# Attention in a fused attention and non-local block: scores and value products in quarter tiles, block by block

## The chip, the cores and the metric

The kernel runs on one core of a Trainium2 chip. A core has TensorE (matrix products, named PE in the profile; its weight loads are PEld), VectorE (DVE), ScalarE (ACT), GpSimd (POOL) and SyncE (SP), whose queue starts most transfers. The metric is the device time of one execution in microseconds.

## The reference

Eight images of 512 channels and 32 x 32 positions (N = 1024) go through two layers, all in 32-bit floats. Layer 0 is attention with 8 heads of 64 channels; layer 1 is a non-local block without softmax, followed by a normalization over the whole batch.

```python
q, k, v = (conv1x1(x, W, b).reshape(B, 8, 64, 1024) for W, b in ((Wq, bq), (Wk, bk), (Wv, bv)))
attn = softmax(einsum('bhdn,bhdm->bhnm', q, k) * 64 ** -0.5)
x = x + conv1x1(einsum('bhnm,bhdm->bhdn', attn, v), Wp, bp)
theta, phi, g = (conv1x1(x, w, b).reshape(B, 256, 1024) for w, b in ...)
y = einsum('bcd,bdn->bcn', einsum('bcn,bdn->bcd', theta, phi) / 1024, g)
z = conv1x1(y, W_w, W_b) + x
out = (z - mean(z)) * rsqrt(var(z) + 1e-5) * gamma + beta     # mean and variance per channel, over the batch
```

## The kernel before

**Products with weights.** Each 1x1 convolution (q, k, v, project, theta with phi, g, and the last product z of the first images) is done as seven block products instead of eight, on quarters of the weight matrix and of the data, with sums and differences of quarters made beforehand. `seven` (line 169) runs them in the order of the table `SEVEN` (line 165): each entry names the weight block, the data block, the PSUM slot 0 to 2 that it adds onto, the output quarter that is read from the slot after it, and whether that read is the first of its quarter (`first`, mostly on ScalarE) or is added to it (`add`, on VectorE). Two entries with one slot accumulate in it, so the second waits until the slot was read. `data_sums` (line 151) makes the data's four sums on VectorE in four blocks of the ring. `load_w` (line 114) loads the next weights, with two weight buffers.

**PSUM.** Three slots of two banks (`s0` to `s2`, pool `psS`) are given out in turn, to `seven` and to the scores. Two slots of one bank (pool `psO`) take the value products, the denominators and a few small products.

**Attention** (line 281). A pair of heads has its 2 x 64 channels on the 128 partitions. A unit is a pair of heads and one half of the 1024 query positions: 8 units. A step is a unit and one of 8 blocks of 128 keys: 64 steps per image. A step's scores (line 303) are two products of 64 channels by 128 keys with 512 queries, one per head, each in one half of the array's rows (tiles of 64 rows x 128 columns), each into its own PSUM bank; ScalarE takes exp of both banks at once into a ring block (line 306), and VectorE adds the block to the unit's running sum (lines 310, 312). A step's value products (lines 335 to 338) are two products of 128 keys by 64 channels with 512 queries, one per head, each in one half of the array's columns (tiles of 128 rows x 64 columns), accumulated over the 8 steps of the unit in one bank, which ScalarE copies out (line 378).

**Order.** The steps are cut into runs of six (`RUN`, the last has four). The order on TensorE is written out by hand (`pe` keeps it): scores of run i, then value products of run i - 1. The first value product of a run is split at column 128 (`LEAD`). The scores of the next image's q (`before_last`) come ahead of the last run's value products, its v (`after_last`) behind the denominators. VectorE, ScalarE and the queues are ordered by a planner that works with its own estimates of durations and when things are due.

**Softmax's denominators.** Of four units the running sums are spread by transfers (`spread`, four of 128 KB per unit) into one tile; VectorE folds it with three additions (`fold`), one product with a matrix of ones (`denominators`) sums it over the partitions, VectorE takes the reciprocal, a transfer to memory and broadcasts bring it back, and VectorE multiplies the four units' outputs with it (`normalize`). The first four units' denominators are done within attention, the other four's after it. In the last image the last four units take a short way each, without spreading (`normalize_alone`: a product with ones, a reciprocal, a multiplication).

**Per image**: attention, v and k of the next image, project with its residual, theta and phi, g, f, z. The first image's q, k and v come ahead of all; the last three images' z, the statistics and the outputs come at the end (`last_z`).

## Time and profile before

| | us |
|---|---|
| median of 3 runs (2222.07 to 2223.56) | 2223.41 |
| the profiled execution's own time | 2223.11 |
| its span, first to last instruction | 2221.3 |
| TensorE busy | 2187.9 |
| VectorE busy | 1285.3 |
| ScalarE busy | 703.3 |
| score products, L303, busy | 462.7 |
| value products, L338, busy | 458.6 |
| exp, L306: 512 of 1.040 | 485.8 |
| additions to the running sums, L312: 384 of 1.225 | 470.3 |

Busy time is the time in which an engine has at least one instruction under way; matmuls overlap, so the mean of one (0.599 for L303) times its count is more than the busy time. A row of the groups gives line, engine, operation, what is written and read, the tile of the array (rows * columns) and the count; a row of the timeline gives start, length and the same. Each product in the program leaves two matmul records and two weight-load records. The granted TensorE clock was 0.994 of full speed in the mean.

### The profile page before, as it was taken

Reading aid. Unit: us, or ns where it says so; the run is one execution under the profiler, and the core shown is the slowest. Engines: PE = TensorE matmul, PEld = TensorE weight load, DVE = VectorE, ACT = ScalarE, POOL = GpSimd, SP = SyncE. Lnnn points to the kernel's source line nnn. Section 1 sums busy time; section 2 is a strip of 40 time slices with the busy share of each in tenths; the row PEclk is TensorE's granted clock in tenths of the full one; section 3 lists DMA queues with packets and bytes.
Section 4 is the critical chain, followed back from the end, with each engine's and each line's share of the span. In section 5 each row is a group of like instructions: output and inputs, shape, how many; then the busy total and the mean of one; then the engine's idle time right before and its main releaser. Section 6 shows DMA issues by size and latency. Waiting matters only on the chain.

```text
span 2221.3 us, 21043 instructions
## 1 busy us (share of the span) xinstructions
PE 2187.9 (98%) x8314; PEld 1111.1 (50%) x8314; DVE 1285.3 (58%) x1231; ACT 703.3 (32%) x823; POOL 35.4 (2%) x36
## 2 busy tenths in 40 slices
PE   8999999999999999999999999999999999999996
PEld 3634664346643456335563355633656346643362
DVE  4576446764477644775447754477543674547736
ACT  1453103531045310452105521065102541045215
POOL 0000000000000000000000000000000000000000
PEclk9999999999999999999999999999999999999998
DMA  6212223122131221412223221232234122132347
GB/s 237 86 24 82 106 100 128 28 76 100 60 128 45 74 86 63 134 43 80 72 92 104 62 67 69 90 105 62 67 129 144 29 62 90 67 106 58 137 159 304
DMA packets 58235, 208.56 MB, mean 94 GB/s; under 512 B 10385, under 2 KB 16785, under 8 KB 52753
## 3 DMA queue, kind: packets, MB, share of 16 engines
q1 hardware_dynamic: 56752, 206.09, 28.0%
q8 instruction: 67, 1.10, 0.2%
q10 hardware_dynamic: 1376, 1.05, 0.1%
q14 instruction: 40, 0.32, 0.0%
HBM read 129.12 MB, written 46.53 MB: 79 GB/s over the span
## 4 chain that ended last, share of the span: by engine, by line
PE 97%; DVE 1%; DMA 0%; ACT 0%; issue 0%; DVEq 0%
PE ps L303 21%; PE po L338 18%; PE pv L189 9%; PE pq L189 9%; PE ptp L189 9%; PE pk L189 9%; PE pp L189 9%; PE pg L189 4%; PE pf L437 2%; PE pz L189 2%; PE pz L536 2%; PE po L336 1%; PE pwf L456 1%; PE po L335 1%; PE den L338 1%; DVE x L485 0%
## 5 line engine op out<-in xcount | busy, mean ns | idle before, releaser
L306 ACT ACTIVATE e<-ps 128x1024 f32<-128x1024 f32 x512 | 485.8, 1040 | 328.1 <-PE ps L303 286.4
L312 DVE TENSOR_TENSOR acc<-acc,e 128x1024 f32<-128x1024 f32 x384 | 470.3, 1225 | 156.5 <-ACT e L306 124.8
L303 PE MATMUL ps<-q,k 64*128 64x512 f32 x2048 | 462.7, 599 | 0.0
L338 PE MATMUL po<-e,v 128*64 128x512 f32 x1872 | 458.6, 595 | 0.0
L303 PEld LDWEIGHTS ps<-q,k 64*128 64x128 f32 x2048 | 187.8, 186 | 272.7 <-issue 164.2
L338 PEld LDWEIGHTS po<-e,v 128*64 128x64 f32 x1872 | 148.0, 137 | 214.9 <-issue 205.7
L446 ACT ACTIVATE g<-pg,gb 128x512 f32<-128x512 f32 x32 | 22.0, 687 | 427.2 <-PE pg L189 427.2
L189 PE MATMUL pp<-t_o,w_WpT 128*128 128x512 f32 x256 | 115.7, 600 | 1.9 <-DVE x L407 1.9
L310 DVE TENSOR_TENSOR acc<-e,e 128x1024 f32<-128x1024 f32 x64 | 77.7, 1214 | 65.4 <-ACT e L306 61.7
L189 PE MATMUL pq<-t_x,w_WqT 128*128 128x512 f32 x256 | 113.9, 593 | 1.5 <-DVE q L206 1.5
L189 PE MATMUL pv<-w_WvT,t_x 128*128 128x256 f32 x512 | 114.5, 379 | 0.0
L189 PE MATMUL ptp<-w_tp,t_x 128*128 128x256 f32 x512 | 114.4, 379 | 0.0
L189 PE MATMUL pk<-t_x,w_WkT 128*128 128x512 f32 x256 | 113.8, 592 | 0.0
L206 DVE TENSOR_TENSOR k<-k,pk 128x1024 f32<-128x1024 f32 x24 | 29.3, 1222 | 143.6 <-PE pk L189 143.6
L189 PEld LDWEIGHTS ptp<-w_tp,t_x 128*128 128x128 f32 x512 | 97.4, 190 | 13.1
L189 PEld LDWEIGHTS pv<-w_WvT,t_x 128*128 128x128 f32 x512 | 97.3, 190 | 13.0
L251 ACT ACTIVATE q<-pq,bq 128x512 f32<-128x512 f32 x64 | 40.5, 683 | 180.3 <-PE pq L189 180.3
L189 PE MATMUL pq<-x,w_WqT 128*128 128x512 f32 x192 | 89.9, 613 | 6.0 <-DMA w_WqT<-in_WqT_dram 6.0
L251 ACT ACTIVATE k<-pk,bk 128x512 f32<-128x512 f32 x64 | 40.5, 683 | 153.6 <-PE pk L189 153.6
L189 PE MATMUL pp<-o,w_WpT 128*128 128x512 f32 x192 | 88.7, 605 | 0.0
L189 PE MATMUL pv<-w_WvT,x 128*128 128x256 f32 x384 | 87.5, 381 | 0.0
L189 PE MATMUL ptp<-w_tp,x 128*128 128x256 f32 x384 | 86.8, 379 | 0.0
(131 smaller groups left out, 2007.0 us busy)
## 6 DMA issues: line engine op xcount, KB each, us to landing
fold<-acc SPq DMA_DIRECT2D x240, 128.0 KB, 2.4
x<-in_x_dram SPq DMA_DIRECT2D x32, 512.0 KB, 5.7
r<-den_d SPq DMA_DIRECT2D x120, 128.0 KB, 3.0
w_WqT<-kept_WqT SPq DMA_DIRECT2D x7, 1792.0 KB, 7.3
w_WvT<-kept_WvT SPq DMA_DIRECT2D x7, 1792.0 KB, 7.3
w_WkT<-kept_WkT SPq DMA_DIRECT2D x7, 1792.0 KB, 6.9
w_WpT<-kept_WpT SPq DMA_DIRECT2D x7, 1792.0 KB, 7.0
w_tp<-kept_tp SPq DMA_DIRECT2D x7, 1792.0 KB, 7.3
```

The source lines that it names most:

```text
L189: pe(nc.tensor.matmul(to_ps, lhsT(k), rhs(k), start=(s, at) not in begun, stop=(k == nk - 1), skip_group_check=True))
L206: nc.vector.tensor_tensor(at, at, ps, ALU.add)
L251: nc.scalar.activation(t[:, c, cols(q)], ps[:, m, :], AF.Identity, bias=bias[:, c:c + 1])
L303: pe(nc.tensor.matmul(ps[:, j, :], k[r, p, m * P:(m + 1) * P], q[r, p, h * 512:(h + 1) * 512], start=True, stop=True))
L306: nc.scalar.activation(e, ps, AF.Exp, scale=SCALE)
L310: nc.vector.tensor_tensor(accs[u], es[u, 0], e, ALU.add)
L312: nc.vector.tensor_tensor(accs[u], accs[u], e, ALU.add)
L335: pe(nc.tensor.matmul(to[:, :LEAD], l, r[:, :LEAD], start=start, stop=False, skip_group_check=True))
L336: pe(nc.tensor.matmul(to[:, LEAD:], l, r[:, LEAD:], start=False, stop=stop, skip_group_check=True))
L338: pe(nc.tensor.matmul(to, l, r, start=start, stop=stop, skip_group_check=True))
L437: pe(nc.tensor.matmul(ps[:, c, :], tp[:, i, c * P:(c + 1) * P], tp[:, i, CI:], start=(i == 0), stop=(i == NB - 1)))
L536: pe(nc.tensor.matmul(ps[:, h, :], wf[:, d, oc * P:(oc + 1) * P], g[d][:, h * 512:(h + 1) * 512], start=(d == 0), stop=(d == IC - 1)))
```

## The change

Scores and value products are both cut into tiles of 64 rows x 64 columns, four products each per step. For the scores the block of 128 keys is cut into two halves (`c`), which go to the two halves of the array's columns; each head keeps its half of the rows and its bank. For the value products the 128 keys are cut into two halves (`r`), which go to the two halves of the rows, each with its own bank; the heads keep their halves of the columns. The two banks of a unit are added at its end: ScalarE copies the first out, VectorE adds the second to it.

There are no runs. For each step TensorE does the scores of step i, then the value products of step i - 2 (`LAG`). All eight PSUM banks form four slots of two banks, given out in turn; in attention, scores use two of them in turn and the units' value products the other two. The small products take the next slot.

The next image's data sums are made near the end of attention, its q after the end, then both denominators, then v, then both normalizations (in order among themselves on VectorE). The fold follows right after the spread of its fourth unit, and the first one ends in a tile of its own (`fold1`); the ring has 10 blocks instead of 11. In the last image, the first four units' denominators and the short ways of the other units stand at steps 46, 54 and 62 and behind the end. `seven` gets a second order (`EARLY`, for the first q and the last project): block product "12" second, the read of "21" started from the slot of "s3t3", and "t4" in a slot of its own.

The diff, without the lines that only rename a pool or a slot:

```diff
-    RUN = 6
-    LEAD = 128
+    LAG = 2
...
-    ring = ctx.enter_context(tc.tile_pool(name="ring", bufs=11))
-    psS = ctx.enter_context(tc.tile_pool(name="psS", bufs=1, space=PSUM))
-    psO = ctx.enter_context(tc.tile_pool(name="psO", bufs=2, space=PSUM))
+    fold1 = ctx.enter_context(tc.tile_pool(name="fold1", bufs=1))
+    ring = ctx.enter_context(tc.tile_pool(name="ring", bufs=10))
+    psum = ctx.enter_context(tc.tile_pool(name="psum", bufs=1, space=PSUM))
...
-    SEVEN = (("11", 0, "11", 0, "11", True), ("s1t1", 3, "t1", 1, "22", True), ("s2t2", 4, "t2", 0, "12", True),
-             ("s4", 6, "22", 1, "12", False), ("s3t3", 5, "t3", 0, "22", False), ("12", 1, "21", 2, "11", False),
-             ("t4", 2, "t4", 0, "21", True))
-
-    def seven(name, w, data, positions_out, first, add, between=None, order=(0, 1, 2, 3, 4, 5, 6)):
+    SEVEN = (("11", 0, "11", 0, (("11", True),)), ("s1t1", 3, "t1", 1, (("22", True),)),
+             ("s2t2", 4, "t2", 0, (("12", True),)), ("s4", 6, "22", 1, (("12", False),)),
+             ("s3t3", 5, "t3", 0, (("22", False),)), ("12", 1, "21", 2, (("11", False),)),
+             ("t4", 2, "t4", 0, (("21", True),)))
+
+    EARLY = (SEVEN[0], SEVEN[5], *SEVEN[1:4], ("s3t3", 5, "t3", 0, (("22", False), ("21", True))),
+             ("t4", 2, "t4", 2, (("21", False),)))
+
+    def seven(name, w, data, positions_out, first, add, between=None, early=False):
 
 
 
         nk, half = w.shape[2], w.shape[3]
         tags = list(free)
+        free[:] = [tags[3], tags[1], tags[0], tags[2]] if early else [tags[3], tags[1], tags[2], tags[0]]
         slots, begun = {}, set()
-        for n, (what, wi, di, s, to, is_first) in enumerate(SEVEN[i] for i in order):
-            if s not in slots:
-                slots[s] = bank(tags[s], f"{name}_{s}")
+        for n, (what, wi, di, s, reads) in enumerate(EARLY if early else SEVEN):
+            if s not in slots or early and what == "t4":
+                slots[s] = bank(tags[s], f"{name}_{s}_{n}")
+                begun -= {one for one in begun if one[0] == s}
             ps, d = slots[s], data[di]
             if positions_out:
                 parts = [(ps.rearrange("p h (i f) -> p (h i) f", f=half)[:, i, :], i * half // 512,
@@ -189,10 +197,10 @@
                     pe(nc.tensor.matmul(to_ps, lhsT(k), rhs(k), start=(s, at) not in begun, stop=(k == nk - 1),
                                         skip_group_check=True))
                     begun.add((s, at))
-            (first if is_first else add)(to, ps)
+            for to, is_first in reads:
+                (first if is_first else add)(to, ps)
...
-        free[:] = [tags[1], tags[2], tags[0]]
...
-                nc.scalar.activation(t[:, c, cols(q)], ps[:, m, :], AF.Identity, bias=bias[:, c:c + 1])
+                if how.get("early") and q == "21":
+                    nc.vector.tensor_scalar(t[:, c, cols(q)], ps[:, m, :], bias[:, c:c + 1], 1.0, ALU.add, ALU.mult)
+                else:
+                    nc.scalar.activation(t[:, c, cols(q)], ps[:, m, :], AF.Identity, bias=bias[:, c:c + 1])
...
+    def columns(ps, lhsT, rhs):
+
+        for j in range(2):
+            pe(nc.tensor.matmul(ps[j * D:(j + 1) * D, :], lhsT, rhs(j), start=True, stop=True, skip_group_check=True))
...
-        def scores(run):
-            for u, m in run:
-                p, h = units[u]
-                ps = next_bank(f"ps_{b}_{u}_{m}")
+        def scores(i):
+            u, m = steps[i]
+            p, h = units[u]
+            ps = bank(tags[i % 2], f"ps_{b}_{u}_{m}")
+            for j in range(2):
+                r = slice(j * D, (j + 1) * D)
+                for c in range(2):
+                    keys = slice(m * P + c * P // 2, m * P + (c + 1) * P // 2)
+                    pe(nc.tensor.matmul(ps[c * P // 2:(c + 1) * P // 2, j, :], k[r, p, keys],
+                                        q[r, p, h * 512:(h + 1) * 512], start=True, stop=True, skip_group_check=True))
+            e = block(f"e_{b}_{u}_{m}")
+            nc.scalar.activation(e, ps, AF.Exp, scale=SCALE)
+            es[u, m] = e
+            if m == 1:
+                accs[u] = w3.tile([P, 2, 512], F32, tag="acc", name=f"acc_{b}_{u}")
+                nc.vector.tensor_tensor(accs[u], es[u, 0], e, ALU.add)
+            elif m > 1:
+                nc.vector.tensor_tensor(accs[u], accs[u], e, ALU.add)
+            if m == NB - 1 and u not in alone:
+                spread(u)
+
+        def weighted(i):
+            u, m = steps[i]
+            p, _ = units[u]
+            if m == 0:
+                sums[u] = bank(tags[2 + u % 2], f"po_{b}_{u}")
+            ps, e = sums[u], es.pop((u, m))
+            for r in range(2):
+                keys = slice(r * P // 2, (r + 1) * P // 2)
                 for j in range(2):
-                    r = slice(j * D, (j + 1) * D)
-                    pe(nc.tensor.matmul(ps[:, j, :], k[r, p, m * P:(m + 1) * P], q[r, p, h * 512:(h + 1) * 512],
-                                        start=True, stop=True))
-                e = block(f"e_{b}_{u}_{m}")
-                nc.scalar.activation(e, ps, AF.Exp, scale=SCALE)
-                es[u, m] = e
-                if m == 1:
-                    accs[u] = w3.tile([P, 2, 512], F32, tag="acc", name=f"acc_{b}_{u}")
-                    nc.vector.tensor_tensor(accs[u], es[u, 0], e, ALU.add)
-                elif m > 1:
-                    nc.vector.tensor_tensor(accs[u], accs[u], e, ALU.add)
-                if m == NB - 1 and u not in alone:
-                    spread(u)
+                    pe(nc.tensor.matmul(ps[j * D:(j + 1) * D, r, :], v[keys, m, (2 * p + j) * D:(2 * p + j + 1) * D],
+                                        e[keys, j, :], start=(m == 0), stop=(m == NB - 1), skip_group_check=True))
+            if m == NB - 1:
+                nc.scalar.copy(part(u), ps[:, 0, :])
+                nc.vector.tensor_tensor(part(u), part(u), ps[:, 1, :], ALU.add)
...
-        def fold(g):
-            t = folded[g]
-            for to, l in ((0, 1), (2, 3), (0, 2)):
-                nc.vector.tensor_tensor(t[:, to, :], t[:, to, :], t[:, l, :], ALU.add)
-
-        def columns(ps, lhsT, rhs, start, stop, lead):
-
-            for j in range(2):
-                to, l, r = ps[j * D:(j + 1) * D, :], lhsT(j), rhs(j)
-                if lead and j == 0:
-                    pe(nc.tensor.matmul(to[:, :LEAD], l, r[:, :LEAD], start=start, stop=False, skip_group_check=True))
-                    pe(nc.tensor.matmul(to[:, LEAD:], l, r[:, LEAD:], start=False, stop=stop, skip_group_check=True))
-                else:
-                    pe(nc.tensor.matmul(to, l, r, start=start, stop=stop, skip_group_check=True))
-
-        def denominators(g):
-
-            ps = psO.tile([P, 512], F32, tag="o", name=f"den_{b}_{g}")
+            if i == 3:
+                t = folded[g]
+                if g == 0:
+                    folded[g] = fold1.tile([P, 1, 1024], F32, tag="fold1", name=f"fold1_{b}")
+                for to, l, r in ((t[:, 0], t[:, 0], t[:, 1]), (t[:, 2], t[:, 2], t[:, 3]),
+                                 (folded[g][:, 0], t[:, 0], t[:, 2])):
+                    nc.vector.tensor_tensor(to, l, r, ALU.add)
...
-                nc.vector.tensor_tensor(part(4 * g + i), part(4 * g + i), r, ALU.mult)
-
-        def normalize_alone(u):
-            ps = psO.tile([P, 512], F32, tag="o", name=f"psum_{b}_{u}")
+                dve(nc.vector.tensor_tensor(part(4 * g + i), part(4 * g + i), r, ALU.mult))
...
-        def weighted(run):
-            lead = True
-            for u, m in run:
-                p, _ = units[u]
-                if m == 0:
-                    sums[u] = psO.tile([P, 512], F32, tag="o", name=f"po_{b}_{u}")
-                ps, e = sums[u], es.pop((u, m))
-                columns(ps, lambda j: v[:, m, (2 * p + j) * D:(2 * p + j + 1) * D], lambda j: e[:, j, :],
-                        m == 0, m == NB - 1, lead)
-                lead = False
-                if m == NB - 1:
-                    nc.scalar.copy(part(u), sums.pop(u))
-                    if u in alone:
-                        normalize_alone(u)
-
-        first = 4 * NB // RUN
-        d = None
-        for i, run in enumerate(runs):
-            scores(run)
-            if i == first + 1:
-                fold(0)
-            if i == first + 4:
+        for i in range(len(steps) + LAG):
+            if i < len(steps):
+                scores(i)
+            if i == len(steps) - 2:
+                near_end()
+            if i >= LAG:
+                weighted(i - LAG)
+            if alone and i in (46, 54, 62):
+                ps = bank(tags[3 - i // 8 % 2], f"psum_{i}")
+                if i == 46:
+                    d = denominators(0, ps[:, 1, :])
+                normalize_alone(i // 8 - 1, ps[:, 0, :])
+            if alone and i == 58:
                 normalize(0, d)
-            if i:
-                weighted(runs[i - 1])
-            if i == first + 2:
-                d = denominators(0)
-        before_last(lambda: None if alone else fold(1))
-        weighted(runs[-1])
-        d = None if alone else denominators(1)
-        after_last()
+        free[:] = tags
         if not alone:
-            normalize(1, d)
-        return o
+            return o, denominators, normalize
+        normalize_alone(7, next_bank("psum_7")[:, 0, :])
+        return o, None, None
...
-        seven(f"pp_{b}", w, data_sums(quarters_of(o), f"o_{b}"), False, first, add_to(xt), between)
+        seven(f"pp_{b}", w, data_sums(quarters_of(o), f"o_{b}"), False, first, add_to(xt), between,
+              early=b == B - 1)
...
-        def before_last(fold):
+        def near_end():
             if not last:
                 nxt["data"] = data_sums(quarters_of(nxt["x"]), f"x_{b + 1}")
-                fold()
-                nxt["q"], nxt["peak_q"] = heads_of(b + 1, "q", weights("WqT"), bq, nxt["data"])
-                load_w(nc.sync)
-
-        def after_last():
-            if not last:
-                nxt["v"] = values(b + 1, weights("WvT"), nxt["data"])
-                load_w(nc.sync)
-
-        o = attention(b, q, k, v, before_last, after_last)
+
+        o, denominators, normalize = attention(b, q, k, v, near_end)
         between = None
         if not last:
-            v = nxt["v"]
+            q, peak_q = heads_of(b + 1, "q", weights("WqT"), bq, nxt["data"])
+            load_w(nc.sync)
+            d = [denominators(g, next_bank(f"den_{b}_{g}")[:, 0, :]) for g in range(2)]
+            v = values(b + 1, weights("WvT"), nxt["data"])
+            load_w(nc.sync)
+            for g in range(2):
+                normalize(g, d[g])
```

## The prediction

> **What bounds the kernel now.** I read the page's busy shares and its chain first, then the TensorE timeline inside attention, then the same image cut into stages, then what TensorE waits for.
>
> ```profile
> PE 2187.9 (98%) x8314; PEld 1111.1 (50%) x8314; DVE 1285.3 (58%) x1231; ACT 703.3 (32%) x823; POOL 35.4 (2%) x36
> PE 97%; DVE 1%; DMA 0%; ACT 0%; issue 0%; DVEq 0%
> PE ps L303 21%; PE po L338 18%; PE pv L189 9%; PE pq L189 9%; PE ptp L189 9%; PE pk L189 9%; PE pp L189 9%; PE pg L189 4%; PE pf L437 2%; PE pz L189 2%; PE pz L536 2%; PE po L336 1%; PE pwf L456 1%; PE po L335 1%; PE den L338 1%; DVE x L485 0%
> ```
>
> TensorE carries 97% of the chain that ended last; the others work beside it. Only TensorE time can move the result. Its timeline around one pair of runs (start, length, operation, count):
>
> ```profile
> 698.80 1.89 PE L338 MATMUL po<-e,v 128*64 128x512 f32 x8
> 700.62 5.42 PE L303 MATMUL ps<-q,k 64*128 64x512 f32 x24
> 705.97 0.32 PE L335 MATMUL po<-e,v 128*64 128x128 f32 x1
> 705.98 0.64 PE L338 MATMUL po<-e,v 128*64 128x512 f32 x1
> 706.13 0.27 PE L335 MATMUL po<-e,v 128*64 128x128 f32 x1
> 706.24 0.49 PE L336 MATMUL po<-e,v 128*64 128x384 f32 x1
> 706.46 0.59 PE L338 MATMUL po<-e,v 128*64 128x512 f32 x1
> 706.56 0.49 PE L336 MATMUL po<-e,v 128*64 128x384 f32 x1
> 706.88 4.46 PE L338 MATMUL po<-e,v 128*64 128x512 f32 x20
> ```
>
> Each matmul leaves two records[...]. In single records inside a run the two tiles' first passes start 7 ns apart (701.151, 701.158), their second passes 0.429 us later, the next block another 0.429 later: one **half** is 0.4292 us, a block of scores or of value products two halves, 0.858. At the borders more goes by: from the last value half (700.087) to the second scores half (701.151) 1.064 instead of 0.858, so 0.206 lost; from the last scores half (705.443) to 706.883 1.440 instead of 1.287, so 0.153 lost. A pair of runs loses 0.36.
>
> Now the image by stages (attention up to its last run; next q; the last run and the denominators; next v):
>
> ```profile
> core 0: us, PE busy (x) PEld busy (x) DVE busy (x) ACT busy (x) POOL busy (x), PEclk, DMA share, GB/s
> 631.30:742.40 111.10, 111.10 (x522) 43.28 (x521) 83.61 (x74) 64.57 (x71) 0.00 (x0) 1.00 0.29 83
> 742.40:766.60 24.20, 24.20 (x58) 10.56 (x56) 13.25 (x12) 3.79 (x6) 0.00 (x0) 1.00 0.10 22
> 766.60:771.10 4.50, 4.50 (x24) 1.69 (x23) 2.65 (x3) 1.85 (x3) 0.00 (x0) 1.00 0.74 264
> 771.10:795.30 24.20, 24.20 (x114) 21.36 (x113) 13.11 (x11) 3.04 (x3) 0.00 (x0) 1.00 0.25 82
> ```
>
> Busy hides the borders (a matmul's record runs 0.16 us past its stream), so I take starts: 631.316 to 795.350 is 164.03 us. At full rate: 256 halves of attention 109.88, four of denominators 1.72, 56 of pq 24.03, 112 pv records at 0.2158 (the rate of ptp, 24.173/112) 24.17; 159.80 in all. **4.24 us per image are lost**, nearly all at borders. Other waits of TensorE:
>
> ```profile
> PE pq L189 <- DMA w_WqT<-in_WqT_dram: 6.0, 1, 6.0
> PE pp L189 <- DVE x L407: 1.9, 1, 1.9
> PE den L338 <- DVE ri L364: 1.8, 1, 1.8
> PE pq L189 <- DVE q L206: 1.5, 1, 1.5
> ```
>
> The last three are the last image's project, its denominators, and image 0's q.
>
> [...] the 512-wide L338 record of tile two starts at 705.98, before L335's second pass at 706.13, which stands ahead of it in the program. Four tiles at once no run here shows.
>
> **The change part by part.**
>
> *Quarter tiles, same halves.* A scores block becomes 4 matmuls of 64x64 tiles, as does a value block: 16 matmul and 16 load records per step instead of 8 and 8. If four tiles run together, a block still takes two halves. Resources, each against something shown. Moving data: 4 x 64 rows at once, as the value run's 2 x 128. PSUM writes: 4 x 64 partitions in two banks; scores now write 2 x 128. Weight loads: 64 columns keep a tile's loader about 55 ns (705.967 to 706.022), so four one after the other are 0.22 of a 0.429 half. Issue: at 650.589 TensorE's queue was empty after a wait, and the first loads of two successive matmuls came at 650.614 and 650.650: 36 ns per matmul, four per block 0.144 of 0.858. Order: a tile's second pass blocks that tile alone; passing one blocked record, as shown, already fills the array in a steady stream (two tiles one half behind the others). Cost taken: 0; bounds 0 to +0.429 per half (only two in flight), nothing below 0 since each tile streams 512 columns as before.
>
> *Borders.* All mode changes inside attention go (9 or 10 pairs, L335 split included). Left per image: into attention (0.1 of it in my window), into pq, into the two denominators between q and v, out of them: 0.1 + 3 x 0.2 = 0.7.
>
> *Start of attention.* Two score slots instead of three: scores(2) needs exp(0). Before, exp(0) began 1.236 after its scores' first matmul (902.724 to 903.960) and took 1.03; loads and matmul follow 0.1 later: ready at 2.37, wanted at 0.1 + 1.72 = 1.82; **+0.5**. Later scores(i) comes two steps (3.43) after scores(i-2), so 1.1 us spare, or 0.5 with the 0.585 output copy in between. Value products run two steps after their exp: not late.
>
> *VectorE, ScalarE, DMA.* ScalarE: 64.6 of 111 us busy. VectorE gains per unit an add of 128x512 from PSUM, at the 0.69 of L357: 8 x 0.7 = 5.5; second fold 3.7 moves in: 83.6 + 9.2 = 92.8 of 110. Cost 0, hidden by TensorE's 110; if that cover fails, see rival B. Normalize(0) (2 reciprocal of 3.36, 8 products) goes behind v: before, denominators at 770.1 gave normalized parts by 787.1; with 8 products about 9 us more, 796 to 800, wanted by project at 819. Its r loads on SP grow from 8 to 16 there, 3.0 us each, two buffers. Ring 11 to 10: value products and accumulation free blocks two to a few steps after exp. 0.
>
> So images 0 to 6: 159.8 + 0.7 + 0.5 = 161.0 instead of 164.03: **-3.0 each, -21.2**.
>
> *Last image*: first scores to ptp 148.11 (1963.43 to 2111.54). After: 109.88 + 5 column pairs x 0.858 = 4.29 + pp 24.03 = 138.2; entry and start 0.6; three mode excursions at steps 46, 54, 62 at 0.36 to 0.4, and the end 0.4: 1.6; at step 46 two reciprocals (6.7 us) read a slot that the value products of step 50 want about 6.2 us later, behind accumulation too: 1 to 3, take 2; leftovers 0.5. 142.9: **-5.2**. In it the early order of project: pp takes 28.01 now, 1.9 of it waiting and 1.7 more at half clock (0.5 for 3.41 us from 2093.995).
>
> *First q*: t4 gets its own slot and need not wait for the read of s3t3: **-1.5**, the row above.
>
> Sum -27.9. The profiled execution took 2223.11 (span 2221.3 and 1.8 around it), the median is 2223.41; from the median **2195.5 us**.
>
> **Rivals.**
>
> A, the sum above: 0.74, range 2186 to 2204 (lower if the start wait and the step-50 stall don't come, -6; half clock after that stall, +1.7, and borders of 0.3, +5 over the kernel).
>
> B, VectorE takes part of it back: a fold waiting for its spreads (2.4 us each) right behind the last one, queued accumulations, or r loads during v hold the slot of s3t3's read. For it: 84% filled in attention[...]. Against: ring of 10 covers some 8 steps, 13.7 us. 1 to 2.5 us per image: 2204 to 2215. 0.11.
>
> C, other side: quarter tiles do not all run at once. Place: every half of attention, 8 x 256 = 2048. If the two tiles that share rows must load in turn with the stream standing, 55 ns: +113, **2308**; two in flight, +879, 3075. It decides from 27.9/2048 = 14 ns per half. For it: no four-tile stretch in the trace. Against: the five resources above. 0.11.
>
> D, no change: the gain stands but scores wait for exp all along, as only two slots remain. A wait of 0.05 us per step (512) would eat 27.9. Against: 0.5 to 1.1 us spare. 2219 to 2228. 0.04.
>
> **Numbers.** About 0.2% (4.4 us) is what a measurement tells from no change. Faster A + B 0.85, same 0.04, slower 0.11. Range 2186 to 2215: A and B but for their ends, 0.8; the slower case lies outside.
>
> **What would show it.** Right: scores and value records of 64x64, four starts within about 30 ns, 0.429 between halves, about 110.5 from first scores to pq, no L335 rows; den between pq and pv. Wrong: halves over 0.443 us (C), gaps before scores with ScalarE as releaser (D) or before s3t3, t4 or first value products with VectorE (B); pp of the last image still near 28; step 50 of the last image stalling over 3 us.

## The result and the profile after

The changed kernel takes 2211.06 us (median of 6 runs, 2207.80 to 2211.89) against 2222.74 for the kernel before (6 runs, 2219.64 to 2226.62): ratio 0.9944, 95% interval 0.9931 to 0.9957. It is faster by 0.56%, or 11.7 us, where 27.9 us were forecast. The direction and the range were right, the size was not.

The page's busy shares and the chain of the changed kernel:

```profile
PE 2166.6 (98%) x12234; PEld 1066.1 (48%) x12234; DVE 1321.1 (60%) x1299; ACT 735.8 (33%) x821; POOL 35.4 (2%) x36
PE 93%; DMA 3%; DVE 2%; issue 1%; ACT 1%; SPq 0%; DVEq 0%; ACTq 0%
```

TensorE still carries the chain, but 7% of it now belongs to others, where it was 3%. Its timeline in the middle of attention (start, length, operation, count):

```profile
630.74 1.04 PE L346 MATMUL po<-e,v 64*64 64x512 f32 x8
631.60 1.04 PE L324 MATMUL ps<-q,k 64*64 64x512 f32 x8
632.46 1.04 PE L346 MATMUL po<-e,v 64*64 64x512 f32 x8
633.32 1.04 PE L324 MATMUL ps<-q,k 64*64 64x512 f32 x8
```

A block of eight records starts every 0.858 us, whether scores or value products. In single records (each product leaves two, called its first and second pass) the first passes of the four tiles start at 631.599, .606, .613 and .619, the second passes 0.429 later: four tiles run together in the 0.429 us that two tiles took before, and nothing is lost between the two kinds of product. The image's stages, attention, next q, the two denominators, next v:

```profile
core 0: us, PE busy (x) PEld busy (x) DVE busy (x) ACT busy (x) POOL busy (x), PEclk, DMA share, GB/s
627.50:738.10 110.60, 110.27 (x1025) 38.97 (x1024) 81.21 (x76) 68.81 (x71) 0.00 (x0) 1.00 0.26 72
738.10:762.30 24.20, 24.20 (x60) 10.56 (x56) 13.17 (x12) 4.38 (x7) 0.00 (x0) 1.00 0.10 22
762.30:764.20 1.90, 1.90 (x9) 0.48 (x8) 1.35 (x2) 1.27 (x2) 0.00 (x0) 1.00 0.62 106
764.20:788.50 24.30, 24.30 (x114) 21.39 (x113) 12.69 (x9) 3.04 (x3) 0.00 (x0) 1.00 0.30 112
```

By starts this is 160.97 us where it was 164.03, in each of the first seven images to within 0.06. So the core of the forecast holds, and the missing 16 us lie elsewhere. From the starts of matmuls in the two profiled executions (spans 2221.3 and 2209.6):

| stage | forecast | measured |
|---|---|---|
| first q | -1.5 | -1.6 |
| images 0 to 6, first scores to next k | -21.2 | -21.5 |
| image 0: bias products and project | 0 | +3.5 |
| k and project in images 1 and 6 | 0 | +1.3 |
| last image, first scores to end of project | -5.2 | +6.3 |
| the rest | 0 | +0.2 |
| sum | -27.9 | -11.8 |

The last image carries 11.5 of the missing us. TensorE there, at steps 46 to 48 and at the end of attention:

```profile
2023.88 1.04 PE L346 MATMUL po<-e,v 64*64 64x512 f32 x8
2024.85 1.08 PE L295 MATMUL psum<-fold,folds 128*64 128x512 f32 x4
2029.73 1.97 PE L295 MATMUL psum<-acc,ones 128*64 128x512 f32 x4 [3.81 <-DVE ri L373]
2031.63 1.99 PE L324 MATMUL ps<-q,k 64*64 64x512 f32 x8
2033.40 1.93 PE L346 MATMUL po<-e,v 64*64 64x512 f32 x8
...
2064.49 2.75 PE L346 MATMUL po<-e,v 64*64 64x512 f32 x24
2072.12 1.98 PE L295 MATMUL psum<-acc,ones 128*64 128x512 f32 x4 [4.88 <-DVE acc L333]
2074.03 5.14 PE L197 MATMUL pp<-o,w_WpT 128*128 128x512 f32 x8
```

Two things are to be seen. TensorE waits twice for VectorE, 3.8 and 4.9 us. And after each wait its products take twice as long: a scores block of 0.86 us takes 1.77 from start to next start (2031.63 to 2033.40). The record of the granted clock has two stretches of half speed here, 6.83 us each, from 2029.2 and from 2070.1. TensorE stood still for the first 0.6 and 2.0 us of them, and the rest cost it half its length: 3.1 and 2.4 us. Before, this image had one stretch, of 3.41 us. What VectorE did at the end:

```profile
2063.14 0.69 DVE L384 TENSOR_TENSOR o<-o,r 128x512 f32<-128x512 f32 x1 [0.85 <-DMA r<-den_d]
2063.75 3.88 DVE L333 TENSOR_TENSOR acc<-acc,e 128x1024 f32<-128x1024 f32 x3
2067.55 3.35 DVE L390 RECIPROCAL ri<-psum 128x512 f32<-128x512 f32 x1
2070.82 1.16 DVE L333 TENSOR_TENSOR acc<-acc,e 128x1024 f32<-128x1024 f32 x1
```

The last column product (a unit's running sum times the matrix of ones) needs the addition at 2070.82, which stands behind the additions that piled up behind a multiplication, and behind unit 6's reciprocal.

### The profile page after: what moved, and what is told of

Its sections match the earlier page's. It is cut to its first block, busy times and chain, and to the rows that moved or that the text cites. A ratio compares the mean times of both kernels' runs of the same rounds, so it can differ in the third digit from the quotient of the medians.

```text
span 2209.6 us, 28905 instructions
## 1 busy us (share of the span) xinstructions
PE 2166.6 (98%) x12234; PEld 1066.1 (48%) x12234; DVE 1321.1 (60%) x1299; ACT 735.8 (33%) x821; POOL 35.4 (2%) x36
## 4 chain that ended last, share of the span: by engine, by line
PE 93%; DMA 3%; DVE 2%; issue 1%; ACT 1%; SPq 0%; DVEq 0%; ACTq 0%
PE ps L324 19%; PE po L346 19%; PE pp L197 9%; PE pq L197 9%; PE ptp L197 9%; PE pv L197 8%; PE pk L197 6%; PE pg L197 4%; PE pf L449 3%; PE pz L197 2%; DMA r<-den_d 2%; PE pz L545 2%; PE pwf L468 1%; PE den L295 1%; ACT e L327 0%
## 5 line engine op out<-in xcount | busy, mean ns | idle before, releaser
L327 ACT ACTIVATE e<-ps 128x1024 f32<-128x1024 f32 x512 | 523.7, 1024 | 390.7 <-PE ps L324 383.1
L324 PE MATMUL ps<-q,k 64*64 64x512 f32 x4096 | 532.4, 591 | 2.6 <-ACT e L327 2.6
L346 PE MATMUL po<-e,v 64*64 64x512 f32 x4096 | 529.5, 590 | 0.0
L324 PEld LDWEIGHTS ps<-q,k 64*64 64x64 f32 x4096 | 155.0, 133 | 291.6 <-issue 278.9
L346 PEld LDWEIGHTS po<-e,v 64*64 64x64 f32 x4096 | 156.7, 133 | 283.9 <-issue 281.2
L384 DVE TENSOR_TENSOR o<-o,r 128x512 f32<-128x512 f32 x60 | 40.8, 689 | 91.0 <-DMA r<-den_d 91.0
L278 ACT COPY v<-pv 128x1024 f32<-128x1024 f32 x32 | 32.4, 1012 | 173.6 <-PE pv L197 173.6
```

What stands on the lines that cost most here:

```text
L278: seven(f"pv_{b}", w, data, True, lambda q, ps: nc.scalar.copy(at(q), as_v(ps)), lambda q, ps: nc.vector.tensor_tensor(at(q), at(q), as_v( ...
L324: pe(nc.tensor.matmul(ps[c * P // 2:(c + 1) * P // 2, j, :], k[r, p, keys], q[r, p, h * 512:(h + 1) * 512], start=True, stop=True, skip_gr ...
L327: nc.scalar.activation(e, ps, AF.Exp, scale=SCALE)
L346: pe(nc.tensor.matmul(ps[j * D:(j + 1) * D, r, :], v[keys, m, (2 * p + j) * D:(2 * p + j + 1) * D], e[keys, j, :], start=(m == 0), stop=(m ...
L384: dve(nc.vector.tensor_tensor(part(4 * g + i), part(4 * g + i), r, ALU.mult))
```

## The experiments

**The theory** after the result: quarter tiles give what was forecast; the loss is the order of the small steps around them, in the last image and in image 0, where TensorE waits for VectorE and then runs at half clock. **Rivals**: VectorE simply has too much to do there; the half clock belongs to the quarter tiles; and the gain comes from the new order rather than from the tiles. All runs were timed beside the kernel before. What is told of stages is read from each run's own profile.

**The tiles of before in the new order.** Scores in 64 x 128, value products in 128 x 64, all else as changed:

```diff
-                for c in range(2):
-                    keys = slice(m * P + c * P // 2, m * P + (c + 1) * P // 2)
-                    pe(nc.tensor.matmul(ps[c * P // 2:(c + 1) * P // 2, j, :], k[r, p, keys], ...
+                pe(nc.tensor.matmul(ps[:, j, :], k[r, p, m * P:(m + 1) * P], ...
...
-            for r in range(2):
-                keys = slice(r * P // 2, (r + 1) * P // 2)
-                for j in range(2):
-                    pe(nc.tensor.matmul(ps[j * D:(j + 1) * D, r, :], v[keys, m, ...], e[keys, j, :], ...
+            for j in range(2):
+                pe(nc.tensor.matmul(ps[j * D:(j + 1) * D, 0, :], v[:, m, ...], e[:, j, :], ...
...
-                nc.vector.tensor_tensor(part(u), part(u), ps[:, 1, :], ALU.add)
```

> Order, slots, lag and all else of the changed kernel, but the tiles of before: scores in 64 x 128, value products in 128 x 64, in one bank, without the addition of a second bank. Theory (the gain of 3.08 us per image comes from mode changes that the quarter tiles spare): each of 512 steps pays two mode changes, 0.36 us together, so 2211 + 184 = about 2395 us. Rival (the gain comes from the order block by block and the slots, and the tiles are beside the point): 2205 to 2225.

Measured: 2375.7 us, 1.0687 of before (1.0669 to 1.0705). Its timeline inside attention:

```profile
700.08 1.08 PE L342 MATMUL po<-e,v 128*64 128x512 f32 x4
701.09 1.13 PE L322 MATMUL ps<-q,k 64*128 64x512 f32 x4
702.15 1.08 PE L342 MATMUL po<-e,v 128*64 128x512 f32 x4
703.16 1.13 PE L322 MATMUL ps<-q,k 64*128 64x512 f32 x4
```

A step takes 2.07 us instead of 1.717: 0.35 for two mode changes (a mode change: TensorE goes from one tile shape to another). Attention is 132.25 us instead of 110.59, 0.338 per step over all 64, a little less than the 0.36 taken. The gain is the tile shape's; the new order with the old tiles costs 7%.

**Quarter tiles two steps at a time.** The same products in another order:

```diff
-            if i < len(steps):
+            if i % 2 == 0 and i < len(steps):
                 scores(i)
-            if i == len(steps) - 2:
-                near_end()
+                if i == len(steps) - 2:
+                    near_end()
+                scores(i + 1)
```

> Quarter tiles as changed, but TensorE does the scores of two steps and then the value products of two steps. Theory (with one tile shape the order makes no difference to TensorE): 2211 plus or minus 3, halves of 0.429 us as before. Rival (block by block is needed, since otherwise scores wait for exp with two slots): a wait of 0.2 us or more per pair of steps, 2260 or more.

Measured: 2207.17 us (0.9932; 0.9915 to 0.9948). Attention takes 110.65 us per image, against 110.59. With one tile shape the order made no difference to TensorE here, and two score slots suffice in both. The 4 us below the changed kernel's median is one more than expected: in this run's profile image 0's project had a half clock of 3.41 instead of 6.83 us, images 1 and 6 had no wait, and the last image took 152.0 us instead of 154.5.

**A slot of its own for the denominators in the last image.**

```diff
+            if alone and i == 38:
+                d = denominators(0, bank(tags[3], f"den_{b}_0")[:, 0, :])
             if alone and i in (46, 54, 62):
                 ps = bank(tags[3 - i // 8 % 2], f"psum_{i}")
-                if i == 46:
-                    d = denominators(0, ps[:, 1, :])
```

> The first four units' denominators of the last image move from step 46, where they share a slot with unit 4's column product, to step 38 and a slot of their own, which no value product wants before step 42. Theory (the shared slot makes TensorE wait 3.8 us for the reciprocal, and the wait halves the clock for 6.8 us): no wait at steps 38 and 46, no half clock after them; the last image's time from first scores to project falls from 128.9 to about 122.3 us, the kernel from 2211.1 to about 2204.5. Rival (VectorE is behind in this image, and TensorE waits for its reciprocals whatever slot they read): the wait goes along to steps 38 to 42, and the time falls by 0 to 2 us.

Measured: 2203.20 us, 0.9913 (0.9899 to 0.9927). TensorE at steps 38 and 46:

```profile
2009.08 1.08 PE L295 MATMUL den<-fold,folds 128*64 128x512 f32 x4
2010.09 1.09 PE L324 MATMUL ps<-q,k 64*64 64x512 f32 x8
...
2016.72 1.09 PE L346 MATMUL po<-e,v 64*64 64x512 f32 x8 [0.39 <-DVE ri L373]
...
2024.61 1.08 PE L295 MATMUL psum<-acc,ones 128*64 128x512 f32 x4
2025.62 1.09 PE L324 MATMUL ps<-q,k 64*64 64x512 f32 x8
```

The wait and the half clock behind it are gone, 0.4 us are left at step 42, and the last image takes 148.3 us instead of 154.5; the wait at the end, 4.6 us, stays. The rival falls: with the same reciprocals, at another step and on different slots, TensorE hardly waits. In the changed kernel the two column products wrote different banks of one slot, and the second waited for the reciprocal that read the first. Two separate tiles at step 46 itself weren't tried, so slot and step are not told apart.

**Less for VectorE near the end.**

```diff
-            if alone and i in (46, 54, 62):
+            if alone and i in (46, 54, 59):
...
-            if alone and i == 58:
+            if alone and i == 50:
                 normalize(0, d)
```

> In the last image unit 6's column product goes from step 62 to step 59, and the first four units' multiplications from step 58 to step 50; the shared slot at step 46 stays. Theory (at the end TensorE waits 4.9 us since VectorE does the reciprocal of unit 6 and four multiplications ahead of the last addition to unit 7's sum, and the wait halves the clock again): the wait before the last column product goes, project runs at full clock in 24.0 to 24.2 instead of 25.6 us, and the kernel falls from 2211.1 to about 2204. Rival (VectorE has too much to do in the last image, whatever the order): the wait stays above 3 us, and the kernel stays above 2208.

Measured: 2206.50 us, 0.9929 (0.9916 to 0.9943). The wait before the last column product shrinks from 4.9 to 2.4 us, and waits of 1.0 at step 58 (unit 7's value products, for unit 5's reciprocal) and 0.6 at step 59 appear; project takes 25.3 us, still partly at half clock. Both expectations missed: the order matters, but half of the wait stayed, so that VectorE's load in this image counts as well.

**All short ways as early as their slots allow.**

```diff
-            if alone and i in (46, 54, 62):
+            if alone and i == 36:
+                d = denominators(0, bank(tags[3], f"den_{b}_0")[:, 0, :])
+            if alone and i == 42:
+                normalize(0, d)
+            if alone and i in (43, 51, 59):
...
-                if i == 46:
-                    d = denominators(0, ps[:, 1, :])
...
-            if alone and i == 58:
-                normalize(0, d)
```

> The last image's short ways as early as their slots allow: the first four units' denominators at step 36 on a slot of their own, their multiplications at step 42, the column products of units 4, 5 and 6 at steps 43, 51 and 59. Theory (the last image loses by order alone: a shared slot at step 46, and reciprocals of 3.36 us that stand in VectorE's queue before what the end needs): from first scores to the end of project 141 to 144 us instead of 154.5, at most one wait of TensorE over 1 us, and the kernel near 2199. Rival (VectorE has about 39 us of work in the last 38 us of attention, so that a wait over 2 us and a half clock stay at the end): above 2202.

Measured: 2200.50 us, 0.9887 (0.9871 to 0.9904). From first scores to the end of project 145.3 us instead of 154.5, no half clock in this image, project 24.14. Waits of 1.3, 1.8 and 1.6 us stay. The rival's half clock did not come, but the stage stayed above the 141 to 144 us of the theory. So most of the loss was order; some 2 us more than hoped for stay as VectorE's lateness, now in three short waits.

**Image 0.** The first four units' denominators back into attention, in this image alone:

```diff
+            if b == 0 and i == 36:
+                d = denominators(0, bank(tags[3], f"den_{b}_0")[:, 0, :])
+            if b == 0 and i == 46:
+                normalize(0, d)
...
-            d = [denominators(g, next_bank(f"den_{b}_{g}")[:, 0, :]) for g in range(2)]
+            late_groups = range(1 if b == 0 else 0, 2)
+            d = {g: denominators(g, next_bank(f"den_{b}_{g}")[:, 0, :]) for g in late_groups}
...
-            for g in range(2):
+            for g in late_groups:
                 normalize(g, d[g])
```

> In image 0 alone, the first four units' denominators go back into attention, to step 36 on a slot of their own, and their multiplications to step 46; the last image stays as changed. Theory (eight multiplications behind v make VectorE late in image 0, where their transfers queue among first-time weight loads, and the bias sums before project wait for it): the column of small products and the first 40 records of project, 25.9 us now, fall to 22.4 to 24, for 0.36 of one more excursion, and the kernel falls by 1.5 to 3. Rival (the first-time weights' own sums or the small products' slots hold it): it stays above 25.

Measured: 2207.80 us, 0.9923 (0.9906 to 0.9939). The bias products and the first 40 records of project take 22.4 us instead of 25.9, and TensorE no longer waits for the bias. Attention of this image pays 1.7 us for it (a wait of 1.3 for the fold, and an excursion to the denominators' tile shape and back), so some 2 us are left. Even those are not sure in size: with image 0 as changed, this stage took 23.8 to 25.9 us in eight profiled executions, by how much half clock followed. In the changed kernel VectorE had stood at these multiplications, the last of them ended at 263.3 where its transfer came late, and the additions to the bias, which project waits for, came at 272.3 instead of partly during the products:

```profile
269.72 0.58 PE L149 MATMUL pbp<-bvc,w_WpT 128*128 128x1 f32 x4
272.54 6.46 PE L197 MATMUL pp<-o,w_WpT 128*128 128x512 f32 x8 [2.24 <-DVE bp L151]
```

**Both moves, and two ways on.**

> Both of the two before. Theory: the sum of the two gains, 2195 to 2198. Rival (the two stalls are one and the same lateness that moves on): no more than the better of the two.

Measured: 2201.29 us (2198.44 to 2203.51), 0.9895 (0.9878 to 0.9911). The profiled execution, the fastest of four, has both gains (span 2196.7, no half clock between 11.5 and 2178.9 us, image 0's bias products and first 40 records of project 20.7 us). The median has not: it is no better than that of the last image's move alone, 2200.5, as the rival said, though not for its reason (see the half clock below). The run with the waits placed later:

```diff
-            if alone and i == 36:
+            if alone and i == 38:
...
-            if alone and i == 42:
+            if alone and i == 44:
...
-            if alone and i in (43, 51, 59):
+            if alone and i in (44, 52, 59):
...
-            if b == 0 and i == 36:
+            if b == 0 and i == 38:
```

> The run with both moves, each standing one to two steps later where its input was late: denominators at step 38 in image 0 and in the last image (the fold came 1.3 us late at step 36), unit 4 at step 44, unit 5 at step 52 (its slot was read 1.8 us late at step 51), unit 6 at 59. Theory (these waits were only early placements): the three waits of 1.3, 1.3 and 1.8 us go, the last image takes 139 to 141 us from first scores to the end of project, the span falls from 2196.7 by 3 to 5 and the median to about 2196, near the 2195.5 forecast for the change. Rival (VectorE is full in the last image, so that a wait removed comes back at the end): the wait before the last column product grows past 3 us, no gain.

Measured: 2200.22 us (2198.34 to 2203.18), 0.9901 (0.9885 to 0.9916). The two waits of 1.3 went, that of 1.8 shrank to 0.8, the one at the end grew from 1.6 to 2.2 and brought 3.41 us of half clock: 146.0 us for the last image. The theory missed, and the rival's 3 us weren't reached: part of what was taken away in front came back behind, and the half clock took the rest.

The next run goes on from this one: what it does in image 0 alone is done in every image but the last.

```diff
-            if b == 0 and i == 38:
+            if not alone and i == 38:
...
-            if b == 0 and i == 46:
+            if not alone and i == 46:
...
-            late_groups = range(1 if b == 0 else 0, 2)
+            late_groups = (1,)
```

> As the run beside it, with the first four units' denominators in attention, at step 38, and their multiplications at step 46, in all images. Theory (the waits of 0.4 to 1.3 us in the next image's k, which came in some images of some runs, are VectorE standing at eight multiplications whose transfers are late): no such wait in any image, for 0.16 us of further mode changes and records per image, within 2 us of the run beside it, with a smaller spread. Rival (these waits have another source): they go on appearing.

Measured: 2205.13 us (2202.78 to 2205.82), 0.9922 (0.9908 to 0.9935). Next k takes 24.03 us in every image, as the theory has it. That is no proof: three other profiled executions, with all eight multiplications behind v, have no wait there either. And it costs more than it saves, about 1 us per image from first scores to next k (161.92 for 160.97), 1.6 in image 6, since step 42's value product waits 0.4 to 1.0 for the denominators' reciprocal, which I had not counted.

The last image of this run is the same code as in the run with the waits placed later, and its wait at the end is the same. Here no half clock follows, and the stage takes 144.2 us instead of 146.0. The last column product, and the two stretches of 3.41 us around it (TensorE's busy time stands behind the comma, the clock third from the right), first with the waits placed later, then here:

```profile
2063.25 1.97 PE L295 MATMUL psum<-acc,ones 128*64 128x512 f32 x4 [2.16 <-DVE acc L333]
2059.78:2063.19 3.41, 1.31 (x16) 0.18 (x8) 3.41 (x4) 0.58 (x1) 0.00 (x0) 1.00 0.94 306
2063.19:2066.60 3.41, 3.35 (x6) 1.16 (x7) 1.85 (x2) 0.00 (x0) 0.00 (x0) 0.50 1.02 396
...
2067.46 1.08 PE L295 MATMUL psum<-acc,ones 128*64 128x512 f32 x4 [2.16 <-DVE acc L333]
2063.65:2067.06 3.41, 1.66 (x16) 0.30 (x8) 3.31 (x4) 0.76 (x2) 0.00 (x0) 1.00 0.96 290
2067.06:2070.47 3.41, 3.00 (x9) 1.27 (x10) 2.75 (x3) 0.00 (x0) 0.00 (x0) 1.00 1.02 381
```

So the length of a wait does not settle what follows it. TensorE is busy for 1.31 us of the first stretch there and for 1.66 us of it here; more on this below. The changed kernel in the same series:

> The changed kernel itself, beside the two runs before on the same chip: 2207 to 2212 us by all theories, half clock in image 0 and twice in the last image.

Measured: 2208.95 us, 0.9942 (0.9929 to 0.9956), with the same two waits (3.8 and 4.8 us). Behind the first, half clock lasts 3.41 us here and not 6.83, and the last image takes 152.6 us instead of 154.5. In this execution images 1 and 6 have no wait in k: that part comes and goes. Of a stage's time in a single execution, some 2 us can be such chance.

**Standstills by themselves.** In images 1 to 6, TensorE is held before project by fills on GpSimd:

```diff
+    still = const.tile([P, 512], F32, tag="still", name="still")
+    nc.vector.memset(still, 1.0)
...
+        if 0 < b < B - 1:
+            ps = next_bank(f"idle_{b}")
+            pe(nc.tensor.matmul(ps[:D, 0, :1], ones, still[:, :1], start=True, stop=True))
+            for _ in range((1, 2, 3, 4, 6, 8)[b - 1]):
+                nc.gpsimd.memset(still, 1.0)
+            pe(nc.tensor.matmul(ps[:D, 0, 1:2], ones, still[:, :1], start=True, stop=True))
```

> The changed kernel with a standstill of TensorE before project in images 1 to 6, by a chain of 1, 2, 3, 4, 6 and 8 fills of 128x512 on GpSimd between two tiny products: about 0.9, 1.4, 2.0, 2.5, 3.6 and 4.8 us. Theory (a standstill of some 2 us or more is followed by half clock for 3.41 or 6.83 us, which costs TensorE as much as half of that): the shortest two leave the clock full, the longest three halve it, each such image loses 1.7 or 3.4 us beyond its standstill, 2234 to 2242 in all. Rival (the half clock comes with the quarter tiles or the mode changes in attention, not with a standstill): no half clock before project in images 1 to 6, about 2226.

Measured: 2234.57 us, one run. Four of the six stretches, from the second tiny product on over project's first 40 records (the third number from the right is the granted clock):

```profile
543.83:561.20 17.37, 17.37 (x42) 7.90 (x43) 9.36 (x12) 0.46 (x1) 0.00 (x0) 1.00 0.29 106
813.90:831.30 17.40, 16.99 (x41) 7.71 (x42) 9.76 (x12) 0.22 (x1) 0.35 (x1) 1.00 0.27 99
1085.20:1104.40 19.20, 19.20 (x44) 8.49 (x44) 8.71 (x11) 0.00 (x0) 0.00 (x0) 0.91 0.19 81
1632.70:1653.00 20.30, 20.30 (x42) 9.06 (x43) 7.01 (x10) 0.00 (x0) 0.00 (x0) 0.85 0.11 46
```

| from last to next matmul start, us | half clock, us | first 40 records of project, us |
|---|---|---|
| 0.84 | none | 17.27 |
| 1.48 | none | 17.27 |
| 2.06 | 3.41 | 18.97 |
| 2.65 | 3.41 | 18.96 |
| 3.81 | 6.83 | 20.04 |
| 4.98 | 6.83 (from 2.7 us into the wait) | 19.35 |

The half clock follows the standstill, with 128x128 tiles too; attention of those images, with all its quarter tiles, keeps the full clock, as in the changed kernel, where the profile has 1.00 from 278.15 to 2029.17 us. The rival on the tiles falls. The theory's 2 us fit these six cases (1.48 us left the clock full, 2.06 us halved it), but where it said 1.7 or 3.4 us lost beyond the standstill, it was 1.7, 1.7, 2.8 and 2.1.

## Why the prediction was right and wrong

**Quarter tiles at the full rate: right.** Four tiles take a half of 0.429 us, and rival C, slower, did not come.

**Borders and the start of attention: right.** 160.97 us against a forecast of 161.0; the wait for exp at the start cost what was taken (the first three score blocks take 3.14 us in images 0 and 1 and 3.19 in the others, some 0.6 more than three blocks, of which 0.5 is the wait). Rival D did not come: scores wait for exp nowhere else.

**First q and the early order: right.** -1.6 for -1.5 (in the other profiled executions of this code 0.8 to 1.8, since a wait of up to 1.4 us for the data's sums comes and goes). Where the clock is full, the last project takes 24.14 us for 28.01.

**The last image: wrong, and this is the step that failed.** The prediction: "at step 46 two reciprocals (6.7 us) read a slot that the value products of step 50 want [...] take 2; leftovers 0.5." I put the stall four steps late. The first to want the slot was the second column product, at once, and it waited 3.8 us. The "leftovers" were a wait of 4.9 us: I had counted VectorE's load over a whole image, 84%, and not over the last third of this one, where four reciprocals of 3.36 us stand among the additions. The sizes: steps 46 to 48 took 11.56 us where two column products, three blocks and an excursion (to another tile shape and back) make 4.66, so 6.9 lost for 2; the end took 35.11 where 27.86 was due, so 7.2 lost for 0.5. Own slot and earlier places together take back 9.1 of it (145.3 us for 154.5).

**The half clock: seen and not priced.** The prediction names the 3.41 us of half clock behind a wait of 1.9 and allows 1.7 for one more. The two waits brought 13.7 us of it, which cost 5.5 us beside the 8.7 us of waiting. In the profiles of the kernel before and of the changed kernel, the changes of the granted clock lie whole multiples of 3.413 us apart. In the changed kernel half clock begins at 271.31, at 2029.18, which is 515 times 3.413 us later, and at 2070.14, 12 times 3.413 us after that; in the kernel before at 274.69 and, 533 times 3.413 us later, at 2093.99.

How long TensorE was busy in the 3.41 us between two points of a run's grid, in stretches that hold a wait for VectorE or a part of one, and what the clock was in the next stretch:

| run, start of the stretch | the wait, us | busy in the stretch, us | clock of the next |
|---|---|---|---|
| before, 2042.79 | 1.79 | 1.62 | 1.00 |
| before, 2090.58 | 1.91 | 1.50 | 0.50 |
| changed, 2025.76 | 3.81 | 0.16 | 0.50 |
| changed, 2066.72 | 4.88 | 0.53 | 0.50 |
| waits placed later, 2059.78 | 2.16 | 1.31 | 0.50 |
| in attention in every image, 2063.65 | 2.16 | 1.66 | 1.00 |

In these six cases 1.50 us or less was followed by half clock and 1.62 us or more was not. That the busy time within one such stretch decides it is an estimate of mine from them. It would explain why a wait of some 2 us can be followed by half clock or not: it can lie in one stretch or be cut by a border. Once the clock is halved, the same work takes twice as long (a scores block 1.77 us for 0.86): in the changed kernel the stretch from 2029.18, 2.86 us busy, was followed by another at 0.50, that from 2032.59, 3.41 us busy, by one at 1.00. The wait of 3.8 us at step 46 was followed by 6.83 us in one execution of the changed kernel and by 3.41 in the other. Busy time alone does not tell it: in the kernel before, TensorE was busy for all 3.41 us from 271.28 with products of a single column, and half clock followed.

**VectorE and the transfers at no cost: wrong in image 0.** The prediction had the multiplications done at 796 to 800, 26 to 30 us behind the denominators, where project wants them at 819. They took 44 to 47 us in all seven images, 27 to 30 us more than before and not "about 9 us more"; the profile has VectorE waiting for transfers between them (in image 0 for 1.46, 1.02 and 1.34 us ahead of the last three). "Cost 0, hidden" still held in images 2 to 5, with about 5 us to spare, and gave 1.3 us away in images 1 and 6 in this execution. In image 0, where VectorE also has the bias additions to do before project, it failed: the multiplications ended at 263.3, the additions came at 272.3, at a cost of 3.5 (1.3 to 3.5 in the executions with this code). That is rival B's mechanism with 4.8 us in all, beside case A rather than in its place.

What stays open: the versions with both moves vary from 2198 to 2203 us. The half clock fits that. The four executions of the first of them took 2198.4, 2199.8, 2202.8 and 2203.5 us with mean granted clocks of 0.996, 0.995, 0.994 and 0.993. Image 0's tiny bias products, some 3.5 us of products of one column, were followed by no half clock (both moves), by 3.41 us (image 0 alone) or by 6.83 us (waits placed later), although TensorE did not wait for the bias in any of the three. Why these three differ is not shown, and only one execution of each version has a trace, so nothing is shown for the others. No order among 2200.2, 2200.5 and 2201.3 us is claimed. All three are faster than both kernels.

## What to carry to other kernels

If two kinds of small products alternate, give them one tile shape: a change of mode cost 0.15 to 0.2 us here, and with one shape the two orders came within 0.06 us per image of each other. When a rewrite moves the small steps at the seams along, price each by its own neighbourhood: which slot it takes, who wants that slot first, and how much the engine that frees it has to do in just those microseconds. A standstill of the bounding engine must be priced with what follows it: a standstill of 2.06 us cost a further 1.7 us here, nearly twice its length in all, and one of 2.16 us was followed by half clock in one run and not in another. And a stage's time from one execution carries that chance, so a second execution should be read beside it.

## What the runs showed of the hardware

In the block of the changed kernel at 631.60 us, four 64 x 64 tiles with f32 operands start 7 ns apart and their second passes follow 0.429 us later; with two tiles of 64 x 128, in the kernel before, a pass of 512 columns takes 0.4292. The first passes of all four start (631.599 to 631.619) ahead of any second pass (from 632.029), although the first product stands whole before the other three in the program.

In the profiles of the two kernels half clock came in stretches of 3.41 or 6.83 us whose borders lie on one grid of 3.413 us; at the very end, where TensorE has no work, it stays (0.50 from 2189.60 to 2209.55 in the changed kernel). A standstill of 2.06 us was followed by it and one of 1.48 us was not (fills on GpSimd); waits of 2.16 us were followed by it in one run (waits placed later) and not in another (denominators in attention in every image). Half clock can begin within a standstill: in the changed kernel it began at 2070.14, in the wait of 4.88 us that ended at 2072.12. Products of a single column, one every 0.112 us from 271.31 to 274.70 in the kernel before, without a wait of TensorE, were followed by 3.41 us of it, as a standstill was.
